# Grid values turned on TensorE instead of by DMA, with the last half chunk of the down projection stacked

## The chip, the cores and the metric

The kernel runs on one core of a Trainium2 chip, in one launch. The metric is device time in microseconds; before, the median of three runs is 670.58 us (665.73 to 671.05). The engines are TensorE (PE; PEld is its weight load), VectorE (DVE), ScalarE (ACT), GpSimd (POOL) and SyncE (SP), which only issues DMAs here. Each takes its own instructions in program order; semaphores tie them together.

## The reference

All tokens (4 batches of 2048, width 256) are normalised; then one branch is a linear attention and the other a gated feed-forward net whose inputs and weights are rounded to FP4 in blocks of 16.

```python
def fp4_quant_dequant(x):
    xb = x.reshape(shape[:-1] + (shape[-1] // BLOCK, BLOCK))
    scale = jnp.maximum(jnp.max(jnp.abs(xb), axis=-1, keepdims=True) / 6.0, 1e-12)
    xn = xb / scale
    idx = jnp.searchsorted(_MID, jnp.abs(xn))
    return (_GRID[idx] * jnp.sign(xn) * scale).reshape(shape)

xn = _layernorm(x)
# attention on xn
Q, K, V = xn @ Wq.T + bq, xn @ Wk.T + bk, xn @ Wv.T + bv
Q, K = Q / norm(Q over tokens), K / norm(K over tokens)
tailor = 1 / (L + Q . (sum(K) + EPS))
s = xn + gamma * (sum(V) + Q (K V)) * tailor
# feed-forward: fp4_linear rounds both operands with fp4_quant_dequant
h = silu(fp4_linear(xn, w_gate)) * fp4_linear(xn, w_up)      # 256 -> 704
g = silu(fp4_linear(h, w_down))                              # 704 -> 256
out = x + s * g
```

## The kernel before

The 8192 tokens are 32 groups of 256 (T = 2 halves of 128 tokens; 8 groups make a batch). The order of the work is written out by hand: the program order is each engine's queue. After a start that also rounds and turns the weights, a loop `for s in range(3, N - 1)` (line 1042) makes 28 passes, each of which works on several groups at once:

- group s+3: gram matrix (`gram_step`), maxima and rounding of its normalised tokens (in `scale_h(s - 1, s + 3)`, together with group s-1), turning of the tokens for the attention (`turn_xn`)
- group s+2: its rounded tokens are scaled back (`rescale_x`, line 488) and split into three parts of a reduced format (`part_a` on ScalarE, `part_b` and `part_m` on VectorE, lines 497 to 511)
- group s+1: gate and up projection in six chunks, each a `gu_begin` (first matmuls, then a scaling copy in PSUM on ScalarE, line 540) and a `gu_end` (last matmuls, Silu, product with up: h). Chunks 0 to 3 have the product on VectorE (`times_up`), 4 and 5 on GpSimd (line 567). The chunks rotate through three PSUM banks
- group s-1: `scale_h` (maxima, reciprocal, product y, lines 163 to 186), `short_part` (three ScalarE copies to 16 bits, line 221), `on_grid` (rounding by a huge addition, line 231)
- group s-2: `rescale_h` (line 513), grid values times scales, in the layout that the down projection needs
- group s-3: `down`, the down projection (line 578), and its Silu `gate_of`
- group s-7: attention output (`preset`, `attend`), one pass later `close` (product with the gate, sum with x) and `store`.

Grid values are made with tokens on partitions, and the next matmul needs them turned. The values and their scales go separate ways. The values: `turn_q` (line 481) has SP issue a DMA transpose of the 16-bit tile into `qt`. The scales: `turn_scales` (line 457) turns them on TensorE, evicts them (`sct`), stores them to DRAM (`there`), and `spread_scales` (line 468) reads them back with each row repeated 16 times, into `se` (128 x 1920, f32, 960 KB, one buffer). `rescale_h` and `rescale_x` multiply `qt` by `se`, on VectorE and on GpSimd. The scales of group s-1 are spread after `rescale_h(s - 2)` has read the old ones.

A group has 1408 h values per token pair (11 chunks of 128; 5.5 per half of the tokens). `down` runs 6 chunks for each half, with the middle chunk in both and half of its weight rows set to zero: 12 matmuls of 128x256 in f32, each of which the profile shows as two instructions.

PSUM tile tag `tp` has two banks for everything that is turned. In every second pass `deviation_steps` yields 13 small VectorE operations (Newton's square root for two groups' deviations, ending in `shiftp`), which `little()` hands out one by one between other work; `normalize(s + 4)` on ScalarE needs them. The attention matrices of a batch are made by a generator, `attention(b)` (line 661), of which `turn()` takes a step at five places of a pass.

Of the kernel before, what the change touches and what calls it, by code (L numbers as in the profile page):

```python
# [9 lines left out]
F32 = mybir.dt.float32  # L10
BF16 = mybir.dt.bfloat16
# [9 lines left out]
BLK = 16  # L21
# [8 lines left out]
def kernel(  # L30
# [31 lines left out]
    P = 128  # L62
# [78 lines left out]
    load_x(4)  # L141
    wd_n = tok.tile([P, NS * P], F32, tag="se", name="wd_n", bufs=1)[:, 0:HF]
    nc.sync.dma_start(
# [6 lines left out]
    ident = const.tile([P, P], F32, tag="ident", name="ident")  # L150
    make_identity(nc, ident)
    nc.gpsimd.memset(wv_sb[:, :, L + 1 : L + 2], 1.0)

# [62 lines left out]
    def grid_tile(y: bass.AP, nm: str):  # L216
        return tok.tile([P, NS * P], F16, tag="t", name=f"t_{nm}", bufs=2)[:, 0 : y.shape[1]]

# [215 lines left out]


    scales, there_sc, spread_sc, turned = {}, {}, {}, {}

# [30 lines left out]
    def spread_scales(key, tag: str = "se"):  # L468
        there, n = there_sc.pop(key)
        most = NS * P if tag == "se" else HF  # L470
        se = tok.tile([P, most], F32, tag=tag, name=f"se_{key}", bufs=1 if tag == "se" else 3)[:, 0 : n * BLK]
        nc.sync.dma_start(
            se,
            there[0:n, :]
            .rearrange("(b g) t -> b (g t)", b=CB)
            .unsqueeze(1)
            .to_broadcast([CB, BLK, n * BLK]),
        )
        spread_sc[key] = se

    def turn_q(n: int, q: bass.AP, tag: str = "qt"):
        F = q.shape[1]
        most = NS if tag == "qt" else NIC
        qt = tok.tile([P, most, P], F16, tag=tag, name=f"qt_{n}", bufs=2 if tag == "qt" else 3)
        nc.sync.dma_start_transpose(qt[:, 0 : F // P, :], q)
        turned[n] = qt.rearrange("p g t -> p (g t)")

    def rescale_x(n: int, key: int):

        f = tok.tile([P, T * L], F32, tag="f", name=f"f_{n}", bufs=2)  # L490
        nc.gpsimd.tensor_tensor(f, turned[key][:, HF:], spread_sc[key][:, HF:], ALU.mult)  # L491
        return f
# [19 lines left out]

    def rescale_h(n: int, lo: int = 0, hi: int = HF, tag: str = "hqt"):
        if lo == 0:
            ht = tok.tile([P, HF], F32, tag=tag, name=f"hqt_{n}", bufs=1 if tag == "hqt" else 3)
            hqt[n] = ht.rearrange("p (g t) -> p g t", t=P)
        ht = hqt[n].rearrange("p g t -> p (g t)")
        nc.vector.tensor_tensor(ht[:, lo:hi], turned[n][:, lo:hi], spread_sc[n][:, lo:hi], ALU.mult)  # L518
        if hi == HF:
            turned.pop(n), spread_sc.pop(n)  # L520

# [54 lines left out]
    hqt, ods = {}, {}  # L576

    def down(n: int, part: int, parts: int = 2, banks=None):

        half = NIC // T  # L580
        t, i = divmod(part, parts)
        if n not in ods:
            ods[n] = ps_od.tile([P, T, L], F32, tag="od", name=f"dn_{n}")
        size = (half + 1) // parts
        for i in range(i * size, (i + 1) * size):
            nc.tensor.matmul(  # L586
                ods[n][:, t, :],
                hqt[n][:, t * half + i, :],
                wdt[:, t * (half + 1) + i, :],
                start=(i == 0),  # L590
                stop=(i == half),
            )

    def gate_of(n: int):
# [66 lines left out]
    def attention(b: int):  # L661
# [7 lines left out]
        nc.tensor.transpose(ps[:, 0:P], S[:, 0, P:L], ident)  # L669
        evict(S[:, 1, 0:P], ps[:, 0:P])  # L670
        u_b = alg.tile([P, L], F32, tag="row", name=f"ub_{b}", bufs=2)
        spread_rows(u_b, S[:, :, L], f"u{b}")
        yield


# [5 lines left out]
        for i, (pool, tag) in enumerate(  # L681
            ((ps_tp, "tp"), (ps_tp, "tp"), (ps_gu, "gu"), (ps_od, "od"))
        ):
# [38 lines left out]
        yield  # L722
        yield


        for t in range(KC):
            nc.vector.tensor_scalar(Q[:, t, :], Q[:, t, :], inv[:, t : t + 1], None, ALU.mult)
        yield
        ps = ps_tp.tile([P, KC, L], F32, tag="tp", name=f"pq_{b}")
# [6 lines left out]
        evict(R, ps)  # L736
        yield
        yield
# [46 lines left out]
        for t, ps in enumerate(pts):  # L785
# [5 lines left out]
            nc.vector.tensor_scalar(MT[:, t, rest], ps[:, rest], tg[:, t : t + 1], None, ALU.mult)  # L791
        yield

        ps = ps_tp.tile([P, KC, L], F32, tag="tp", name=f"pM_{b}")
# [49 lines left out]

    wdt = const.tile([P, NIC + 1, L], F32, tag="wdt", name="wdt")

    def turn_d(wdz):
        half = NIC // T
        H = P // 2
        ends = small.tile([P, KC, P], F32, tag="ends", name="ends", bufs=1)  # L850
        w3 = wdz.rearrange("p (t f) -> p t f", t=KC)
        nc.scalar.copy(ends[:, :, 0:H], w3[:, :, FF - H : FF])
        nc.scalar.copy(ends[:, :, H:P], w3[:, :, 0:H])
        nc.gpsimd.memset(wdt[H:P, half, :], 0.0)
        nc.gpsimd.memset(wdt[0:H, half + 1, :], 0.0)
        for i in range(0, NIC - 1, 2):
            tp = ps_tp.tile([P, 512], F32, tag="tp", name=f"tp_d{i}")
            at = [i + k if i + k < half else i + k + 2 for k in range(2)]
            for k in range(2):
                f0 = at[k] * P if at[k] < half else (at[k] - half - 2) * P + H  # L860
                for t in range(KC):
                    nc.tensor.transpose(
                        tp[:, k * L + t * P : k * L + (t + 1) * P], w3[:, t, f0 : f0 + P], ident
                    )
            if at[1] == at[0] + 1:
                evict_over_one(wdt[:, at[0] : at[0] + 2, :].rearrange("p i n -> p (i n)"), tp)
            else:
                for k in range(2):
                    evict_over_one(wdt[:, at[k], :], tp[:, k * L : (k + 1) * L])
            yield  # L870
        tp = ps_tp.tile([P, 512], F32, tag="tp", name="tp_d")
        for t in range(KC):
            nc.tensor.transpose(tp[:, t * P : (t + 1) * P], ends[:, t, :], ident)
        evict_over_one(wdt[0:H, half, :], tp[0:H, 0:L])
        evict_over_one(wdt[H:P, half + 1, :], tp[H:P, 0:L])
        yield
# [116 lines left out]
    turn_xq(4, rounded(s_x, tx))  # L993
    turn_q(0, on_grid(th, "h0"))
    next(parts)
# [11 lines left out]
    turn_scales(1)  # L1007
    rescale_h(0)
    spread_scales(1)
    turn_q(1, on_grid(th, "h1"))  # L1010

# [10 lines left out]
    def close(f: int):  # L1022
        gated(f, ready.pop(f))
        finish(f, nc.vector)

# [16 lines left out]
    for s in range(3, N - 1):  # L1042
# [11 lines left out]
        turn()  # L1054
        u0 = gu_begin(*pairs[0])
        if s % 2 and s > 3 and s + 4 < N:
            small_ones = deviation_steps()
        sums = sums_of(s + 6)
        for h in late:
            times_up(h)  # L1060
        if parts_x:
            xs = rescale_x(s + 2, s - 2)
        y_h = scale_h(s - 1, s + 3)
        little()
        th = grid_tile(y_h, f"h{s - 1}")
# [24 lines left out]
        if s > 3:  # L1090
            turn_scales(s - 1)
        u2 = gu_begin(*pairs[2])
        if s == 3:
            h1 = gu_end(u1)
            shorts()
        little()
        little()
        if s > 3:
            h1 = gu_end(u1, 1 in DIRECT)
        times_up(h1)  # L1100
        little()
        turn()
        down(s - 3, 0 if s == 3 else 2)
        down(s - 3, 1 if s == 3 else 3)
        q = on_grid(th, f"h{s - 1}")
        little()
        turn_q(s - 1, q)
        if f >= 0:
            preset(f)
        u3 = gu_begin(*pairs[3])  # L1110
        if s == 3:
            down(0, 2)
            down(0, 3)
            turn_scales(2)
        gate_of(s - 3)
        h2 = gu_end(u2, s > 3 and 2 in DIRECT)
        times_up(h2)
        little()
        u4 = gu_begin(*pairs[4])
        h3 = gu_end(u3, s > 3 and 3 in DIRECT)  # L1120
        if parts_x:
            part_a(s + 2, xs)
        times_up(h3)
        little()
        rescale_h(s - 2)
        little()
        spread_scales(s - 1)
        if parts_x:
            part_b(s + 2, xs)
            part_m(s + 2, xs)  # L1130
        little(20)
        if f >= 0:
# [30 lines left out]
    for i in range(f + 3, N):  # L1163
        x_last[i] = x_sb[i]
    y_h = scale_h(n - 1)
    for i in range(5):
# [4 lines left out]
    attends(f)  # L1171
    rescale_h(n - 2, tag="h")
    spread_scales(n - 1)
    turn_q(n - 1, on_grid(th, f"h{n - 1}"))
    downs(n - 2)
# [6 lines left out]
    spread_scales(n, "h")  # L1182
    turn_q(n, on_grid(th, f"h{n}"))
    attends(f + 3, f + 4)
    preset(f + 5, *banks[0])
    rescale_h(n - 1)
    close(f + 1)
    close(f + 2)
# [8 lines left out]
    attends(f + 6, f + 7)  # L1197
    rescale_h(n, 0, (NIC // T + 1) * P, tag="h")
    rescale_h(n, (NIC // T + 1) * P)
    close(f + 5)  # L1200
# [50 lines left out]
```

## Time and profile before

| | us |
|---|---|
| median of three runs | 670.58 |
| the profiled execution, run | 673.65 |
| its span | 671.9 |
| TensorE busy, matmul / weight load | 610.2 / 494.4 |
| VectorE / ScalarE / GpSimd busy | 478.2 / 397.0 / 146.9 |
| granted TensorE clock, mean | 0.979 |

The page shows one profiled execution. "Busy" is the time in which an engine executes; a matmul's end is modelled. A group of instructions is written as line, engine, operation, result <- sources, shapes, count, then busy time, mean ns of one, and idle time before it with what ended it. Four groups that the change touches:

```profile
L586 PE MATMUL dn<-wdt,hqt 128*128 128x256 f32 x768 | 180.4, 379 | 0.5 <-ACT gate L1207 0.5
...
L491 POOL TENSOR_TENSOR f<-qt,se 128x512 f32<-128x512 f16 x27 | 35.4, 1312 | 199.0 <-DMA se<-there 114.0
...
L518 DVE TENSOR_TENSOR hqt<-qt,se 128x1408 f32<-128x1408 f16 (+2 forms) x33 | 53.0, 1607 | 15.1 <-DMA qt<-t_h 15.1
```

Matmuls overlap, so the 379 ns of a `dn` instruction are longer than the distance of two starts.

### The profile page before, as it was taken

To read this page: it belongs to the slowest core of one execution; us is meant where nothing else is said; L and a number is where in the kernel's file an instruction comes from. 1 tells how busy PE (TensorE), PEld (TensorE's weight loads), DVE (VectorE), ACT (ScalarE), POOL (GpSimd) and SP (SyncE) were. 2 spreads that over 40 slices of the span, in tenths; PEclk is the share of its full clock that TensorE was granted. 3 is DMA by queue.
4 is the path that set the end of the run, shared out by engine and by line. 5 is a ranking of instruction groups with operands and counts; after the bars stand their busy time and mean duration, and the time that the engine had idled before them with its cause. 6 is when DMAs were issued, how large, how long until landed. Compare 5 with 4: busy or idle time off the path is not lost.

```text
span 671.9 us, 8659 instructions
## 1 busy us (share of the span) xinstructions
PE 610.2 (91%) x2805; PEld 494.4 (74%) x2807; DVE 478.2 (71%) x915; ACT 397.0 (59%) x1033; POOL 146.9 (22%) x224
## 2 busy tenths in 40 slices
PE   4899996898899999998899999998899999999997
PEld 2445564677778787777778787877778888787785
DVE  6667667584867777687867777687767777687763
ACT  2467847555567676745567685745658575644520
POOL 5467638211011111101012111110111111110000
PEclk9799997897999999999999999999999999999999
DMA  9210475423545756436545656547535545534585
GB/s 211 75 33 16 53 103 128 88 53 77 106 99 123 143 132 142 115 87 136 111 108 124 144 127 141 114 109 131 106 98 128 128 106 125 120 95 96 144 125 135
DMA packets 85513, 74.47 MB, mean 111 GB/s; under 512 B 63228, under 2 KB 69596, under 8 KB 85468
## 3 DMA queue, kind: packets, MB, share of 16 engines
q1 hardware_dynamic: 85196, 73.66, 51.3%
q8 instruction: 22, 0.36, 0.3%
q10 hardware_dynamic: 272, 0.26, 0.1%
q14 instruction: 23, 0.19, 0.1%
HBM read 48.57 MB, written 10.27 MB: 88 GB/s over the span
## 4 chain that ended last, share of the span: by engine, by line
PE 64%; DVE 17%; ACT 10%; DMA 4%; issue 4%; POOL 2%; SPq 0%; ACTq 0%; DVEq 0%; POOLq 0%
PE dn L586 22%; PE gu L536 19%; PE gu L550 6%; PE at L624 5%; PE gram L392 5%; DVE hqt L518 3%; DMA qt<-t_h 3%; PE px L686 2%; DVE xq L510 2%; ACT si L560 2%; ACT gu L540 2%; ACT xn L367 2%; DVE y_h L186 2%; DVE xq L504 2%; DVE scs L163 1%
## 5 line engine op out<-in xcount | busy, mean ns | idle before, releaser
L536 PE MATMUL gu<-wgu,xq 128*128 128x512 f32 (+1 forms) x640 | 185.5, 412 | 7.0 <-ACT xq L499 5.2
L586 PE MATMUL dn<-wdt,hqt 128*128 128x256 f32 x768 | 180.4, 379 | 0.5 <-ACT gate L1207 0.5
L540 ACT ACTIVATE gu<-gu 128x512 f32<-128x512 f32 (+1 forms) x160 | 89.2, 557 | 139.6 <-PE gu L536 139.0
L586 PEld LDWEIGHTS dn<-wdt,hqt 128*128 128x128 f32 x768 | 143.8, 190 | 22.6 <-issue 1.4
L536 PEld LDWEIGHTS gu<-wgu,xq 128*128 128x128 f32 x640 | 116.3, 191 | 29.7 <-ACT xq L499 5.4
L571 DVE TENSOR_TENSOR h<-si,gu 128x256 f32<-128x256 f32 x108 | 45.4, 420 | 119.8 <-ACT si L560 119.6
L567 POOL TENSOR_TENSOR h<-si,up 128x192 f32<-128x192 f32 (+1 forms) x84 | 64.5, 773 | 258.6 <-ACT up L566 241.3
L550 PE MATMUL gu<-wgu,xq 128*128 128x512 f32 (+1 forms) x320 | 99.6, 392 | 0.4 <-ACT gu L540 0.4
L560 ACT ACTIVATE si<-gu 128x256 f32<-128x256 f32 (+1 forms) x192 | 70.0, 364 | 28.2 <-PE gu L536 19.2
L491 POOL TENSOR_TENSOR f<-qt,se 128x512 f32<-128x512 f16 x27 | 35.4, 1312 | 199.0 <-DMA se<-there 114.0
L392 PE MATMUL gram<-xn 128*128 128x257 f32 (+1 forms) x256 | 52.3, 350 | 18.9 <-ACT xn L367 18.9
L392 PEld LDWEIGHTS gram<-xn 128*128 128x128 f32 x256 | 45.6, 203 | 31.4 <-ACT xn L367 23.5
L221 ACT ACTIVATE t_h<-y_h 128x704 f16<-128x704 bf16 (+2 forms) x86 | 60.8, 769 | 10.2 <-DVE y_h L186 9.6
L550 PEld LDWEIGHTS gu<-wgu,xq 128*128 128x128 f32 x320 | 59.5, 189 | 9.6 <-ACT gu L540 1.1
L518 DVE TENSOR_TENSOR hqt<-qt,se 128x1408 f32<-128x1408 f16 (+2 forms) x33 | 53.0, 1607 | 15.1 <-DMA qt<-t_h 15.1
L624 PE MATMUL at<-M,xnt 128*128 128x256 f32 x256 | 63.6, 378 | 0.0
L536 PE MATMUL gu<-wp,xqt 128*128 128x512 f32 (+1 forms) x120 | 52.9, 588 | 2.8 <-ACT xqt L379 2.2
L186 DVE SCALAR_TENSOR_TENSOR y_h<-h,inv_h 128x1408 f32<-128x1408 f32 x32 | 52.9, 1652 | 1.1
L624 PEld LDWEIGHTS at<-M,xnt 128*128 128x128 f32 x256 | 47.9, 189 | 6.2
L163 DVE TENSOR_REDUCE scs<-h 128x88 f32<-128x1408 f32 x32 | 51.6, 1612 | 0.0
L367 ACT ACTIVATE xn<-x,shiftp,rstdp 128x256 f32<-128x256 f32 x46 | 25.4, 604 | 31.5 <-DVE shiftp L343 31.5
L536 PEld LDWEIGHTS gu<-wp,xqt 128*128 128x128 f32 x120 | 22.9, 199 | 24.7 <-issue 16.5
(166 smaller groups left out, 742.1 us busy)
## 6 DMA issues: line engine op xcount, KB each, us to landing
se<-there SPq DMA_DIRECT2D x27, 960.0 KB
x<-in_L_attn_x_dram SPq DMA_DIRECT2D x32, 256.0 KB
out_dram<-gate SPq DMA_DIRECT2D x31, 256.0 KB
xl<-in_L_attn_x_dram SPq DMA_DIRECT2D x27, 256.0 KB
se<-there SPq DMA_DIRECT2D x5, 704.0 KB
there<-sct SPq DMA_DIRECT2D x27, 60.0 KB
wd_n<-in_L_ffn_w_down_dram SPq DMA_DIRECT2D x1, 704.0 KB
wgu_n<-in_L_ffn_w_up_dram SPq DMA_DIRECT2D x2, 256.0 KB
```

What stands on the lines that cost most here:

```text
L163: nc.vector.tensor_reduce(sc, src.rearrange("p a (n k) -> p a n k", k=BLK), AX.X, ALU.max, apply_absolute_value=True)
L186: nc.vector.scalar_tensor_tensor(y.rearrange("p (a n k) -> p a n k", a=a, k=BLK), src.rearrange("p a (n k) -> p a n k", k=BLK), DOWN, inv. ...
L221: nc.scalar.activation(t[:, lo:hi], upper[:, lo:hi], AF.Copy, scale=ONE * (1.0 + 2.0**-8))
L392: nc.tensor.matmul(grams[b][:, o : o + L + 1 - c * P], xn[:, t, c * P : (c + 1) * P], xn[:, t, c * P : L + 1], start=(g == 0 and t == 0 an ...
L518: nc.vector.tensor_tensor(ht[:, lo:hi], turned[n][:, lo:hi], spread_sc[n][:, lo:hi], ALU.mult)
L536: nc.tensor.matmul(gu[:, : nb * P], x_k, w_k, start=(k == 0), stop=(k == len(pairs) - 1), skip_group_check=True)
L540: nc.scalar.activation(gu[:, : nb * P], gu[:, : nb * P], AF.Copy, scale=1.0 + 1.0 / STEP)
L550: nc.tensor.matmul(gu[:, : nb * P], xqt[n][2][:, t, c, :], wgu[2][:, c, cols], start=False, stop=(c == KC - 1), skip_group_check=True,)
L560: nc.scalar.activation(si[:, :nb, :], pair[:, :, 0, :], AF.Silu)
L567: nc.gpsimd.tensor_tensor(h, si[:, :nb, :], up[:, :nb, :], ALU.mult)
L586: nc.tensor.matmul(ods[n][:, t, :], hqt[n][:, t * half + i, :], wdt[:, t * (half + 1) + i, :], start=(i == 0), stop=(i == half),)
L624: nc.tensor.matmul(ready[n][:, t, :], xnt[n][:, c, t * P : (t + 1) * P], M[:, c, :], start=False, stop=(c == KC - 1), skip_group_check=True,)
```

## The change

DMA transposes are gone. `turn_chunks` turns up to eight 128x128 chunks of the 16-bit grid values on TensorE into a `tp` bank, and `rescale_x` and `rescale_h` read them from PSUM; `rescale_x` thereby moves from GpSimd to VectorE. `turned[n]` now holds the untransposed tile.

```diff
-    def turn_q(n: int, q: bass.AP, tag: str = "qt"):
...
-        nc.sync.dma_start_transpose(qt[:, 0 : F // P, :], q)
-        turned[n] = qt.rearrange("p g t -> p (g t)")
+    def turn_chunks(q: bass.AP, g0: int, g1: int, nm: str) -> bass.AP:
+        tp = ps_tp.tile([P, 1024], BF16, tag="tp", name=f"tp_q{nm}_{g0}")
+        for g in range(g0, g1):
+            o = (g - g0) * P
+            nc.tensor.transpose(tp[:, o : o + P], q[:, g * P : (g + 1) * P].bitcast(BF16), ident16)
+        return tp[:, 0 : (g1 - g0) * P].bitcast(F16)
...
-        nc.gpsimd.tensor_tensor(f, turned[key][:, HF:], spread_sc[key][:, HF:], ALU.mult)
+        nc.vector.tensor_tensor(f, turn_chunks(turned[key], NIC, NS, f"x{n}"), spread_sc[key][:, HF:], ALU.mult)
...
+    def rescale_h(n: int, tag: str = "hqt"):
...
+        for g0, g1 in ((0, 8), (8, NIC)):
+            cols = slice(g0 * P, g1 * P)
+            nc.vector.tensor_tensor(
+                ht[:, cols], turn_chunks(q, g0, g1, f"h{n}"), spread_sc[n][:, cols], ALU.mult
+            )
```

`se` has two buffers. `down` runs five whole f32 chunks for each half of the tokens; the middle chunk's two halves are split by `part_middle` into a short part and its rest, stacked over each other (`both`), and multiplied by two 128x256 weight tiles `wde` of the reduced format: 10 f32 matmuls and 4 of the reduced format in place of 12.

```diff
+    def part_middle(n: int, engine):
...
+        for t in range(T):
+            nc.scalar.activation(both[sides[t], t, :], middle[sides[t], :], AF.Copy, scale=SHORT)
+        for t in range(T):
+            engine.tensor_tensor(
+                both[sides[1 - t], t, :],
+                middle[sides[t], :],
+                both[sides[t], t, :].bitcast(F32),
+                ALU.subtract,
+            )
+        over_lower[n] = both
...
+        if i == half - 1:
+            for k in range(2):
+                nc.tensor.matmul(
+                    ods[n][:, t, :],
+                    over_lower[n][:, t, :],
+                    wde[:, k, t, :],
...
-        finish(f, nc.vector)
+        finish(f, nc.gpsimd)
```

In the loop, the scales are spread right after they were turned; `rescale_x` stands before `scale_h`, as before, but now on VectorE; the parts and the Newton steps come earlier. Pass 3 keeps the later places for the parts.

```diff
         u0 = gu_begin(*pairs[0])
+        if s > 3:
+            part_middle(s - 3, nc.gpsimd)
...
-        if parts_x:
+        if parts_x and s > 3:
             xs = rescale_x(s + 2, s - 2)
         y_h = scale_h(s - 1, s + 3)
-        little()
+        little(3)
...
         if s > 3:
             turn_scales(s - 1)
+            spread_scales(s - 1)
         u2 = gu_begin(*pairs[2])
...
-        little()
-        little()
+        little(3)
         if s > 3:
             h1 = gu_end(u1, 1 in DIRECT)
+        if parts_x and s > 3:
+            part_a(s + 2, xs)
         times_up(h1)
-        little()
+        little(2)
         turn()
...
         q = on_grid(th, f"h{s - 1}")
-        little()
-        turn_q(s - 1, q)
+        little(20)
+        turned[s - 1] = q
...
         times_up(h2)
-        little()
+        if parts_x and s > 3:
+            part_b(s + 2, xs)
+            part_m(s + 2, xs)
         u4 = gu_begin(*pairs[4])
         h3 = gu_end(u3, s > 3 and 3 in DIRECT)
-        if parts_x:
+        if parts_x and s == 3:
+            xs = rescale_x(s + 2, s - 2)
             part_a(s + 2, xs)
         times_up(h3)
-        little()
         rescale_h(s - 2)
-        little()
-        spread_scales(s - 1)
-        if parts_x:
+        if parts_x and s == 3:
             part_b(s + 2, xs)
             part_m(s + 2, xs)
-        little(20)
```

In `attention`, the spreading of u moves one step later, the pauses around Q, R and M are placed anew, and the four tiles of px take od, gu, tp, tp in place of tp, tp, gu, od. After the loop `rescale_h` of the last group is one call, and `part_middle` runs on VectorE after each `rescale_h`. `turn_d` builds `wde` from the two half chunks of the weights instead of zero-padded rows.

## The prediction

> **What bounds the kernel now.** I read the page's busy shares first, then the waits, then the chain of waits and the timeline of two middle passes of the loop (503 to 538 us), then the DMA rate by stretches.
>
> ```profile
> PE 610.2 (91%) x2805; PEld 494.4 (74%) x2807; DVE 478.2 (71%) x915; ACT 397.0 (59%) x1033; POOL 146.9 (22%) x224
> ```
>
> ```profile
> POOL f L491 <- DMA se<-there: 114.0, 16, 9.4
> ...
> PE gram L392 <- ACT xn L367: 18.9, 11, 6.9
> ```
>
> TensorE is the wall: 91% busy, and in the chain of waits its pieces lie end to end. The gram of one pass starts at 520.29 and the next at 538.05, 17.76 us, of which 1.29 us is idle before the second; so a pass without a gap is 16.47 us of TensorE. That gap comes in every second pass (nine of 1.23 to 1.31 us, 11.6 us in sum), behind the Newton steps, which VectorE ends after rescale_h and the parts. The first line of the waits (who waited for what: us in all, times, longest) is the one that I build on: GpSimd waits 114 us in all for the spread scales `se`, and it costs nothing, because GpSimd is 22% busy and the parts of x are wanted only at the end of the pass.
>
> ```profile
> 518.36 0.62 SPq L472 DMA_DIRECT2D se<-there  x1
> 519.04 0.45 SPq L649 DMA_DIRECT2D out_dram<-gate  x1
> 519.54 0.42 SPq L108 DMA_DIRECT2D xl<-in_L_attn_x_dram  x1
> 527.61 0.34 SPq L465 DMA_DIRECT2D there<-sct  x1
> ```
>
> ```profile
> 512.23 1.16 POOL L491 TENSOR_TENSOR f<-qt,se 128x512 f32<-128x512 f16 x1 [5.92 <-DMA se<-there]
> ```
>
> The scales of this pass left for DRAM at 527.61; `se` is issued only after the old one has been read. GpSimd's f at 512.23 was released by the `se` issued at 500.42: 11.8 us. The same difference over the sixteen waits runs from 11.40 us (issue 126.17, start 137.57) to 12.30 us (399.88, 412.18).
>
> ```profile
> 525.00:529.00 4.00, 4.00 (x20) 3.39 (x19) 3.02 (x10) 3.86 (x10) 0.00 (x0) 1.00 0.54 122
> 93.00:98.00 5.00, 5.00 (x20) 3.48 (x19) 3.45 (x5) 2.12 (x5) 0.00 (x0) 1.00 0.53 120
> ```
>
> The last two figures are DMA share and GB/s. With little else in flight `se` moves at 120 to 122 GB/s; at that rate its 960 KB (983 kB) take 8 us, whatever else is quiet.
>
> **TensorE's own sum.** *Down projection*: 24 instructions a group become 20, and 4 single-pass ones of 256 columns are added. The old ones take 0.216 us each (six in 1.29 to 1.30 in the chain): minus 0.86. The gate/up matmuls in the same format take 0.93 for four of 512 columns and 0.70 for four of 384, so 0.116 for 256: plus 0.47; at worst the weight load's 0.19 each: plus 0.76. I take minus 0.40. *Turning the grid values*: 15 transposes a pass. Nearest row: tp_xn, four 4-byte 128x128 transposes in 0.44 us, 0.11 each, taken as the upper end; half of it, 0.055, if two bytes halve the passes. I take 0.07: 1.05 us (0.83 to 1.65). Pass: 16.47 - 0.40 + 1.05 = 17.1 us (16.9 to 18.0).
>
> The Trainium skill ("TensorE: Matmul & The Clock Gate", Part 4: PE-mode transpose) gives about 275 ns for a 16-bit 128x128 transpose inside a kernel, and speaks against this change: by it the 15 would be an estimated 4.1 us and the pass 20.2. The rows here say 0.11 for a wider type, and I go by the rows.
>
> **The other moves.** Newton steps: the eight that stood before rescale_h or later now end after on_grid, so shiftp is there before normalize; the gaps of 11.6 us go. Attention gaps (eleven waits on Q, MT and xnt from 129 to 630 us) are 19 us in sum; between none and all goes, I take 12. close's second add (0.69 us on VectorE) goes to GpSimd, at 1.2 to 2 us by its own 128x512 rows; what is behind it there is the next h product, which came 9 us after the gate's product (525.79, 534.86), so it costs nothing; without that gap it would delay h by its own length. rescale_x goes to VectorE: GpSimd's row is 1.18, VectorE's product with one PSUM operand of 128x512 is 0.68, of 128x256 is 0.42; I take 0.7. rescale_h in two pieces costs one more start, by the rows of 512 and 1408 columns (0.69, 1.62) 0.16 us. part_middle: two ScalarE copies of 64x128, below the 0.27 of the 120x128 row, and two small GpSimd products; about 0.5 us of ScalarE, which has 4 us free in a pass. part_a/b/m are the same instructions earlier. VectorE thus stays at about 14 of 17 us in busy time; the trouble is order, not load.
>
> **The new wait.** rescale_x stands at the head of VectorE's pass, before scale_h, and VectorE takes its queue in order. It needs the `se` that was issued in the pass before, and that issue needs: scale_h of that pass (VectorE, behind its own rescale_x), the three short copies (ScalarE), the scales' eviction (behind them on ScalarE), the trip to DRAM, and `se`. Every pass therefore contains one whole round:
> - rescale_x: 0.7
> - scale_h, from the reduction's start (519.81) to the end of y_h's first part (523.25 + 1.62): 5.06
> - ScalarE from the first short copy (525.43) to the end of sct (527.31 + 0.27): 2.15
> - `there` to the next issue on SP: 1.55 at 637.67 to 639.22, 2.00 at 102.35 to 104.35; I take 1.6
> - `se` from issue to use: 11.4 to 12.3. In the new order of SP, store, x and xl follow it at once, as at 518.36, so the rows apply. I take 11.4, the lowest of the sixteen, since no transposes share the engines any more. Alone: the 704 KB one issued at 639.22 was through by about 646.5 (1.8 us to start, then about 130 GB/s); 983 kB at that rate give 9.4, the lower end
> - hand-overs: 0.2
>
> Sum: 21.1 us a pass (19.1 with `se` alone, 22.0 at 12.3), against TensorE's 17.1. Queued behind the waiting rescale_x are scale_h, h0, gated and every later VectorE step; behind y_h on ScalarE stand the scaling copy and si of the next chunks, so TensorE stops at tp_sc and at the second end of a chunk. TensorE's 4 us of slack then hides transposes, attention and gaps: gain and loss on TensorE no longer count. The second buffer of `se` lets the issue go some 6 us earlier, but the use moves up by more: f started at 530.09 in a pass whose u0 began at 519.36, 10.7 us in; it now stands about 1.2 us in.
>
> The Trainium skill ("DMA: Bandwidth & Descriptors", Rules for kernel authors) says to issue a DMA early and wait for it late. The rows agree in kind: a late wait on an idle engine cost nothing here for 114 us.
>
> **Sum against the profiled execution** (span 671.9, run 673.65, which is 0.5% above the median 670.58). Start: with the DMA transposes gone SP is free (their issues took 6.75 and 2.85 us), the scales of group 2 can leave at 97.4 instead of 102.35, `se` lands near 109.5, and tp_sc of pass 4 comes 3.2 us later (0.7 + 2.46 from reduction to scaled maxima): 112.7, before 115.3. From there 25 passes to tp_sc of pass 29 took 597.13 - 115.3 = 481.8 (19.3 each, attention included); at 21.1 they take 527.5. So 45.7 - 2.6 = 43.1 more. Tail: for the last three groups the transposes stand on TensorE right where hqt was ready before: 3 x 0.77; twice the rescaling (1.8) has no cover (n-2 before its down, n before its down); less 4 x 0.4 saved: plus 4.3. 671.9 + 47.4 = 719.3 span, 721.1 run, **718** on the scale of the median.
>
> **Rivals.**
> 1. *`se` lands uncontended* (9.4): round 19.1. tp_sc 29 at 590.2; the attention passes, 22.1 us before with 5.8 us of gaps in three, stay TensorE-bound near 20.7 and add about 16. Time 606.2 - 597.1 + 4.3 more, **684** by the median. For it: share 0.54 leaves room beside `se`. Against: all sixteen rows, with the same neighbours.
> 2. *The round does not bind; the change is faster.* It decides where `se` lands within 7.4 us of its issue (17.1 less the 9.7 of the other steps). Then 671.9 - 11.6 (Newton) - 12 (attention) - 5 (the 5.17 us gap at 106, behind a DMA transpose) + 28 x 0.43 (transposes at 0.055) + 4.3 = 660, **659** by the median; 667 with transposes at 0.07 and half of the attention gaps left. For it: 704 KB took 7.3 us in the tail, and the removed transposes were most of the small packets. Against: 122 GB/s in stretches without transposes.
> 3. *TensorE's transposes are dear* (0.11 or above): pass 18.0; hidden under 21.1, and in rival 2's case 28 x 1.25 in place of 28 x 0.43 makes 681.
>
> **Chances.** Round binds, contended 0.55 (718; 700 to 742); uncontended 0.20 (684); round does not bind 0.20 (659, of which a third ends within 1%); dearer than 742 0.05. Faster by over 1% 0.15, within 1% (about what a measurement can tell) 0.07, slower 0.78. The range reaches into rival 2 at 660 and up to 742.
>
> **What would show it.** Right: VectorE's f waits on DMA se<-there in nearly every pass, 3 to 5 us each; gram to gram 19 to 22 us in plain passes; TensorE below 87% with idle before tp_sc; the gram<-xn gaps gone. Wrong: f released by the transposes on TensorE, `se` landing under 8 us, passes of 17 us. A 0.25 us spacing of the new transposes would show the third rival.

## The result, and the profile after

After takes 733.59 us (median of 4 runs, 732.69 to 736.31) against 670.65 us before: the ratio is 1.0964, with a 95% interval of 1.0905 to 1.1022. The profiled execution took 733.18 us, its span is 731.3 us, the mean granted clock 0.972.

The page of after: first the busy line, then the shares of the chain that ended last by engine and by line, then three groups (line, engine, operation, result <- sources, shapes, count, then busy us, mean ns of one, and idle time ahead with its releaser).

```profile
PE 639.2 (87%) x3267; PEld 512.4 (70%) x3269; DVE 472.5 (65%) x950; ACT 419.0 (57%) x1100; POOL 167.6 (23%) x283
...
DMA 36%; PE 28%; DVE 26%; ACT 7%; issue 3%; POOL 1%; DVEq 0%; SPq 0%; ACTq 0%; POOLq 0%
...
L498 DVE TENSOR_TENSOR f<-tp_qx,se 128x512 f32<-128x512 f16 x27 | 18.7, 692 | 130.6 <-DMA se<-there 120.5
...
L526 DVE TENSOR_TENSOR hqt<-tp_qh,se 128x1024 f32<-128x1024 f16 x64 | 53.9, 883 | 21.3 <-PE tp_qh L492 21.3
...
L616 PE MATMUL dn<-wdt,hqt 128*128 128x256 f32 x640 | 159.9, 392 | 2.7 <-DVE hqt L526 2.2
```

TensorE is busy 29 us more than before, but the span is 59 us longer: its share falls from 91% to 87%. Little of the 29 us is added work: x_columns_first (below) has the same matmuls and is busy 614.2 us, at a mean granted clock of 0.999. The chain of before, over its whole span, was TensorE for 64%:

```profile
PE 64%; DVE 17%; ACT 10%; DMA 4%; issue 4%; POOL 2%; SPq 0%; ACTq 0%; DVEq 0%; POOLq 0%
```

Now it is TensorE for 28%, and 36% go to DMA and 26% to VectorE. VectorE has no more to do than before (472.5 against 478.2 us); it stands still for 130.6 us ahead of one instruction a pass, `f`.

The waits of after (who waited for what: us in all, times, longest):

```profile
DVE f L498 <- DMA se<-there: 120.5, 22, 7.2
ACT t_h L227 <- DVE y_h L188: 93.9, 25, 6.6
...
PEld tp_sc L468 <- issue: 49.0, 16, 4.8
PE tp_sc L468 <- DVE scs L174: 46.3, 16, 4.7
```

The first line is the wait that GpSimd had before, for nearly the same sum (114.0 us), now on VectorE. The others are those who wait for VectorE: ScalarE for `y_h`, TensorE for the scaled maxima. These sums overlap and are not added.

The chain of after from 394.76 to 415.96 us (start, us, what; pieces of one engine left out):

```profile
382.83 11.83 DMA se<-there
...
394.76 0.69 DVE f L498
395.45 2.13 DVE scs L165 x2
...
397.86 0.92 DVE inv_h L178
...
398.80 2.23 DVE y_h L188 x2
...
404.28 11.59 DMA se<-there
...
415.96 0.69 DVE f L498
```

This is one whole round: `f` to `f` in 21.20 us, and over half of it is one transfer. What SP does between, from its timeline (start, us, operation):

```profile
402.64 0.34 SPq L472 DMA_DIRECT2D there<-sct  x1
404.28 0.60 SPq L479 DMA_DIRECT2D se<-there  x1
404.98 0.42 SPq L690 DMA_DIRECT2D out_dram<-gate  x1
405.45 0.41 SPq L100 DMA_DIRECT2D x<-in_L_attn_x_dram  x1
405.91 0.45 SPq L108 DMA_DIRECT2D xl<-in_L_attn_x_dram  x1
```

Between `y_h` and the store lie ScalarE's short copies and the eviction (400.46 to 402.62); the trip to DRAM takes 1.64 us. From the `f` of pass 4 (112.65) to that of pass 29 (651.59) 25 rounds take 538.94 us, 21.56 each.

### The profile page after: what moved, and what is told of

The parts are those of the page before. It is cut to its first block, busy times and chain, and to the rows that moved or that the text cites. A ratio compares the mean times of both kernels' runs of the same rounds, so it can differ in the third digit from the quotient of the medians.

```text
span 731.3 us, 9674 instructions
## 1 busy us (share of the span) xinstructions
PE 639.2 (87%) x3267; PEld 512.4 (70%) x3269; DVE 472.5 (65%) x950; ACT 419.0 (57%) x1100; POOL 167.6 (23%) x283
## 4 chain that ended last, share of the span: by engine, by line
DMA 36%; PE 28%; DVE 26%; ACT 7%; issue 3%; POOL 1%; DVEq 0%; SPq 0%; ACTq 0%; POOLq 0%
DMA se<-there 35%; PE gu L545 10%; DVE scs L165 6%; PE dn L616 6%; DVE y_h L188 5%; PE at L665 3%; DVE inv_h L178 3%; DVE f L498 2%; PE gu L559 2%; ACT t_h L227 2%; DVE h L580 1%; DVE isq_yp L347 1%; PE pa L788 1%; ACT si L569 1%; PE tp_qh L492 1%
## 5 line engine op out<-in xcount | busy, mean ns | idle before, releaser
L545 PE MATMUL gu<-wgu,xq 128*128 128x512 f32 (+1 forms) x640 | 183.9, 410 | 6.6 <-DVE h L580 5.9
L616 PE MATMUL dn<-wdt,hqt 128*128 128x256 f32 x640 | 159.9, 392 | 2.7 <-DVE hqt L526 2.2
L616 PEld LDWEIGHTS dn<-wdt,hqt 128*128 128x128 f32 x640 | 124.8, 199 | 24.1 <-issue 2.9
L576 POOL TENSOR_TENSOR h<-si,up 128x192 f32<-128x192 f32 (+1 forms) x84 | 56.9, 681 | 247.6 <-ACT up L575 247.5
L559 PE MATMUL gu<-wgu,xq 128*128 128x512 f32 (+1 forms) x320 | 104.4, 408 | 1.6 <-ACT gu L549 1.1
L498 DVE TENSOR_TENSOR f<-tp_qx,se 128x512 f32<-128x512 f16 x27 | 18.7, 692 | 130.6 <-DMA se<-there 120.5
L682 POOL TENSOR_TENSOR gate<-gate,xl 128x512 f32<-128x512 f32 x27 | 34.5, 1280 | 224.6 <-issue 199.1
L526 DVE TENSOR_TENSOR hqt<-tp_qh,se 128x1024 f32<-128x1024 f16 x64 | 53.9, 883 | 21.3 <-PE tp_qh L492 21.3
L398 PE MATMUL gram<-xn 128*128 128x257 f32 (+1 forms) x256 | 50.2, 340 | 8.3 <-ACT xn L373 8.3
L398 PEld LDWEIGHTS gram<-xn 128*128 128x128 f32 x256 | 42.3, 195 | 14.5 <-ACT xn L373 9.0
L468 PE MATMUL tp_sc<-ident,scs 128*120 128x128 f32 (+1 forms) x32 | 9.7, 304 | 46.3 <-DVE scs L174 46.3
```

Source lines behind the costliest of these rows:

```text
L398: nc.tensor.matmul(grams[b][:, o : o + L + 1 - c * P], xn[:, t, c * P : (c + 1) * P], xn[:, t, c * P : L + 1], start=(g == 0 and t == 0 an ...
L526: nc.vector.tensor_tensor(ht[:, cols], turn_chunks(q, g0, g1, f"h{n}"), spread_sc[n][:, cols], ALU.mult)
L545: nc.tensor.matmul(gu[:, : nb * P], x_k, w_k, start=(k == 0), stop=(k == len(pairs) - 1), skip_group_check=True)
L559: nc.tensor.matmul(gu[:, : nb * P], xqt[n][2][:, t, c, :], wgu[2][:, c, cols], start=False, stop=(c == KC - 1), skip_group_check=True,)
L576: nc.gpsimd.tensor_tensor(h, si[:, :nb, :], up[:, :nb, :], ALU.mult)
L616: nc.tensor.matmul(ods[n][:, t, :], hqt[n][:, t * (half + 1) + i, :], wdt[:, t * half + i, :], start=(i == 0), stop=False, skip_group_chec ...
```

## The experiments

| kernel | us, median | ratio to before, 95% interval |
|---|---|---|
| after | 733.6 | 1.0964 (1.0905 to 1.1022) |
| before_x_on_vector | 871.5 | 1.3016 (1.2971 to 1.3060) |
| x_after_scale | 662.1 | 0.9890 (0.9848 to 0.9933) |
| x_columns_first | 654.6 | 0.9776 (0.9747 to 0.9806) |
| neighbours_early | 717.9 | 1.0722 (1.0690 to 1.0753) |
| sixteen_rows | 667.4 | 0.9965 (0.9934 to 0.9996) |
| x_first_turned_twice | 680.5 | 1.0175 (1.0139 to 1.0210) |
| x_first_old_down | 663.1 | 0.9917 (0.9888 to 0.9945) |
| x_first_newton_old | 669.2 | 0.9984 (0.9957 to 1.0011) |
| x_first_and_after | 659.5 | 0.9847 (0.9822 to 0.9872) |
| before_newton_early | 649.7 | 0.9694 (0.9677 to 0.9711) |
| dma_turned_old_down | 642.2 | 0.9587 (0.9555 to 0.9620) |
| dma_turned_stacked | 637.8 | 0.9524 (0.9498 to 0.9550) |

The theory: `rescale_x` at the head of VectorE's pass makes a round through `se`, and this alone makes after slower than before. The rivals: the transposes on TensorE, the stacking or the moved steps.

### Is it the place of rescale_x?

**before_x_on_vector** changes one word of before: `rescale_x` runs on VectorE. No transposes, no stacking, one buffer for `se`.

```diff
-        nc.gpsimd.tensor_tensor(f, turned[key][:, HF:], spread_sc[key][:, HF:], ALU.mult)
+        nc.vector.tensor_tensor(f, turned[key][:, HF:], spread_sc[key][:, HF:], ALU.mult)
```

> The kernel before with one word changed: rescale_x on VectorE in place of GpSimd, everything else as it was, DMA transposes included. Theory: here se is issued only after rescale_h, so the round is longer than in the changed kernel: rescale_x 0.7, from scale_h's start to rescale_h's end 11.2 (its VectorE work) to 15.5 us (502.79 to 518.29 in the trace before), se 11.8: 24 to 28 us a pass against 19.3, and 790 to 900 us. If the wait for se costs nothing because later work hides it (rival), the kernel loses at most VectorE's 0.7 us a pass, 27 x 0.7 = 19: 670 to 690 us.

871.5 us. Its waits:

```profile
ACT t_h L221 <- DVE y_h L186: 225.4, 28, 17.2
DVE f L491 <- DMA se<-there: 223.2, 26, 12.0
```

The wait that was free on GpSimd costs 202 us on VectorE. It is more than in after because, with one buffer, the next `se` is issued only behind `rescale_h`: in the middle of the trace `hqt` starts at 510.71, the issue is at 512.36, `f` at 524.32. A round takes 26.84 us on average here (`f` at 121.89 to `f` at 792.91) and 21.56 in after: the change's second buffer and its early spreading win back a good part of what its own move costs. The granted clock is also lower, 0.894 and 0.902 in the two runs for 0.984 to 0.989 in before's beside them; how much of the 202 us is TensorE at that clock is not shown.

**x_after_scale** is after, with two lines exchanged.

```diff
+        y_h = scale_h(s - 1, s + 3)
         if parts_x and s > 3:
             xs = rescale_x(s + 2, s - 2)
-        y_h = scale_h(s - 1, s + 3)
```

> The changed kernel with two lines exchanged: rescale_x stands behind scale_h in VectorE's queue. If the round over the spread scales sets the pass (theory), it is cut: scale_h, the short copies and the issue of se no longer wait for the se before. TensorE then sets a plain pass: 16.47 - 0.39 + 15 x 0.057 = 16.9 us, and with the attention's extra work 18.2 to 18.6 on average, so the time falls by 25 x 3 to 25 x 3.4, to 648 to 660 us. If TensorE's added transposes, or the clock it loses in its gaps, make the change slow (rival), the exchange moves nothing there: 715 to 735 us.

662.1 us, just above what was expected, 71 us below after. From its waits, and two neighbouring grams of TensorE's timeline:

```profile
DVE f L498 <- DMA se<-there: 2.3, 4, 1.0
```

```profile
356.21 1.53 PE L398 MATMUL gram<-xn 128*128 128x257 f32 x8
...
373.25 1.53 PE L398 MATMUL gram<-xn 128*128 128x257 f32 x8
```

`f` hardly waits for `se`; TensorE is 94% busy, and its plain passes (gram to gram) take 17.05 us. scale_h no longer stands behind the wait of its own pass, only behind that of the pass before. So a round through `se` has two passes to run in, and no longer sets their length. The order of the two lines is worth more than the whole loss of 63 us.

**x_columns_first** leaves the order and makes the transfer short: the 512 columns that `f` needs are read first, by a DMA and into a tile of their own.

```diff
+        if n * BLK > HF:
+            sx = tok.tile([P, T * L], F32, tag="sx", name=f"sx_{key}", bufs=2)
+            nc.sync.dma_start(sx, rows[:, HF:].unsqueeze(1).to_broadcast([CB, BLK, T * L]))
+            spread_x[key] = sx
...
+        nc.sync.dma_start(se, rows[:, 0:HF].unsqueeze(1).to_broadcast([CB, BLK, HF]))
```

> The changed kernel with se read in two DMAs: the 512 columns for x first, into a tile of their own, then the 1408 for h. rescale_x keeps its place ahead of scale_h. Theory: only the landing in the round gets shorter: 256 KB at 122 GB/s, 2.1 us, and some 2 to 3 to start and end, so 4 to 5 in place of 11.7; the round is 9.5 + 4 to 5 = 13.5 to 14.5 us, below TensorE's 16.9, and the time is that of the exchanged order, 648 to 662 us. If the order of VectorE itself were at fault and not the landing (rival), it stays above 710 us.

654.6 us. The timeline of VectorE in a plain pass, and the wait for `f` in the list:

```profile
350.67 0.69 DVE L496 TENSOR_TENSOR f<-tp_qx,sx 128x512 f32<-128x512 f16 x1 [1.91 <-PE tp_qx L490]
```

```profile
DVE f L496 <- PE tp_qx L490: 46.4, 22, 2.8
```

`f` is released by TensorE's transposes now, in step with a pass of 17.05 us. The issue of `sx` was at 343.13, so the scales were there within 7.5 us; whether in the 4 to 5 us expected can't be seen from a wait that TensorE ended. TensorE is the wall again, and the kernel is 2.2% faster than before.

### Why does the read take 11.7 us?

**neighbours_early** issues the store and the loads of x and xl from ScalarE's queue, ahead of its short copies, so that they don't follow `se`.

```diff
-        load_x(s + 7)
-        reload_x(s - 7)
...
+            load_x(s + 7, nc.scalar)
+            reload_x(s - 7, queue=nc.scalar)
+            store(nc.scalar)
...
-        store()
```

> The changed kernel with the loads of x and xl and the store issued from ScalarE's queue just ahead of the short copies, when se has landed and the next one is not yet issued; the round itself is untouched. If the three neighbours stretch se's landing (part of the theory), it falls from 11.7 to 9.4 to 9.9 us, the pass from 21.6 to 19.3 to 19.8, and the time by 25 x 1.8 to 25 x 2.3, to 676 to 690 us (three more issues stand on ScalarE, outside the round or with 1.5 us inside it: then up to 715). If se is slow by its own shape alone (rival), the landing stays above 11 us and the time within 10 us of 733.

717.9 us, between theory and rival: a miss for both. `se`, issued at 417.71, is used at 428.42: 10.7 us, 1 us less than with neighbours. The stretches of that transfer (window, then busy us of PE, PEld, DVE, ACT and POOL with counts, granted clock, DMA share, GB/s):

```profile
420.00:425.00 5.00, 5.00 (x31) 4.38 (x30) 2.73 (x5) 3.63 (x13) 0.65 (x2) 1.00 0.51 114
425.00:427.00 2.00, 2.00 (x13) 1.79 (x12) 0.00 (x0) 1.36 (x4) 1.27 (x3) 1.00 0.56 123
427.00:428.40 1.40, 1.40 (x8) 1.13 (x7) 0.00 (x0) 0.30 (x1) 0.17 (x1) 1.00 0.01 0
```

Two things stand here. The windows count a packet (one piece of a transfer) where it starts; by the trace's packets the last of `se` ends at 427.37, and another 1.05 us pass before `f` starts. And a lone `se` keeps the sixteen DMA engines only half busy, 0.51 to 0.56.

**sixteen_rows** follows the second. The read repeats 8 rows of DRAM 16 times; here the scales are stored twice, and 16 rows are repeated 8 times. The same bytes land in the same tile.

```diff
-        there = dram.tile([NS * CB, P], F32, tag="there", name=f"there_{key}")
-        nc.sync.dma_start(there[0:n, :], st[0:n, :])
+        there = dram.tile([2 * CB, NS, P], F32, tag="there", name=f"there_{key}")
+        copies = there.rearrange("(b c) g t -> c b g t", c=2)
+        for c in range(2):
+            nc.sync.dma_start(copies[c][:, 0 : n // CB, :], st[0:n, :])
...
-            .to_broadcast([CB, BLK, n * BLK]),
+            .to_broadcast([2 * CB, BLK // 2, n * BLK]),
```

> After, with the turned scales stored twice, so that the read of se is 16 outer rows repeated 8 times in place of 8 rows repeated 16 times: the same bytes into the same tile. In stretches with se alone the DMA engines are busy 0.51 to 0.55 of sixteen at 114 to 123 GB/s, as if eight of them carried it. Theory: they do (the Trainium skill, DMA: Bandwidth & Descriptors, Rules for kernel authors, says that an outermost dimension below 16 confines a DMA to so many engines), so the read moves at up to twice the rate. 983 kB then take some 4 us of moving for 8, se is there 7.7 to 9 us after its issue for 11.7, the second store adds 0.4, the round is 17.4 to 19 and the time 640 to 680 us. Rival: the rate is that of the one source row or of the queue, the share means something else: se still 11 us or more, 725 to 745 us.

667.4 us: 66 us off after, with rescale_x where the change put it and the whole `se` in one read. SP, and the stretches of the read, of this kernel:

```profile
384.65 1.34 SPq L474 DMA_DIRECT2D there<-sct  x2
387.63 0.56 SPq L481 DMA_DIRECT2D se<-there  x1
```

```profile
387.60:389.40 1.80, 1.80 (x18) 1.70 (x18) 1.64 (x4) 0.78 (x3) 0.00 (x0) 1.00 0.32 102
389.40:391.00 1.60, 1.60 (x11) 1.50 (x10) 1.60 (x4) 1.03 (x4) 0.03 (x1) 1.00 1.04 254
391.00:392.00 1.00, 1.00 (x8) 0.93 (x7) 0.41 (x1) 0.97 (x4) 0.57 (x1) 1.00 1.02 230
```

`f` starts at 394.19: 6.6 us after the issue, where after needs 11.7, and all the engines are busy. In the trace a packet of `se` takes about as long in both kernels, 0.58 us (neighbours_early) and 0.52 us at the median; but some 8 are under way at a time there and some 16 here, and the whole read moves in 4.4 us for 8.3. So the read ran on eight of the sixteen because its outermost dimension was 8. The Trainium skill ("DMA: Bandwidth & Descriptors", Rules for kernel authors) states it: an outermost dimension below 16 confines a DMA to at most that many engines. The runs agree: 0.51 and 114 GB/s with 8 rows, 1.04 and 254 with 16. The second store is dearer than expected: from the first store to the issue of `se` it is 2.98 us against 1.64. The round is then 17.4 us (394.19 to 411.62), still 0.4 above TensorE's pass of 17.05, and `f` still waits:

```profile
DVE f L500 <- DMA se<-there: 47.1, 16, 4.1
```

### What do the other parts cost?

Next to x_columns_first, where TensorE is the wall, parts of the change can be priced.

**x_first_turned_twice** does each transpose of grid values twice, into the same place.

```diff
-        for g in range(g0, g1):
+        for g in list(range(g0, g1)) * 2:
```

> The version with the x columns of the scales read first (654.6 us), with every transpose of the grid values done twice into the same place. Theory: TensorE is the wall there and a transpose costs what the chain shows, 0.057 us, so 15 more a pass are 0.86 us and 28 passes with the tail about 26 us: 674 to 686, plain passes of 17.9 us. Rival (transposes are dearer than their spacing shows, 0.11 or more each): 700 or above, passes of 18.7 us or more.

680.5 us, 25.9 more, with plain passes of 17.89 us. A line of TensorE's timeline in after and one in this kernel (11 transposes and 22):

```profile
405.54 0.79 PE L492 MATMUL tp_qh<-ident,t_h 128*128 128x128 bf16 x11
406.17 1.08 PE L665 MATMUL at<-M,xnt 128*128 128x256 f32 x4
```

```profile
555.03 1.40 PE L490 MATMUL tp_qh<-ident,t_h 128*128 128x128 bf16 x22
556.27 1.08 PE L663 MATMUL at<-M,xnt 128*128 128x256 f32 x4
```

Start to start: 0.63 us for 11 and 1.24 for 22, 0.057 and 0.056 each; the pass says (17.89 - 17.05) / 15 = 0.056.

**x_first_old_down** undoes the stacking.

```diff
-        for i in range(i * size, min((i + 1) * size, half)):
+        for i in range(i * size, (i + 1) * size):
...
-        if i == half - 1:
-            for k in range(2):
...
-    wde = const.tile([P, 2, T, L], F32R, tag="wde", name="wde")
```

> The version with the x columns of the scales read first (654.6 us), but with the down projection as before: 12 f32 matmuls of 256 columns a group, no part_middle, the zero-padded weight rows. Theory: TensorE is the wall again in this version, so the stacking is worth its matmuls, 24 x 0.216 - (20 x 0.216 + 4 x 0.117) = 0.39 us a group, 32 groups 12.5 us: 664 to 670 us. Rival: the stacking is hidden or eaten by the parts it adds, 652 to 658.

663.1 us, 8.5 more and just under the range; the plain pass is 17.43 us, 0.38 more. The pass agrees with 0.39; the medians are 4 us short of 12.5. The start is one part of this: the split weight tiles add gaps of 1.07, 0.64 and 0.58 us on TensorE, which this kernel hasn't but for one of 0.49, and a gram that starts at 124.22 in x_columns_first starts at 122.71 here. Where the rest goes is not shown: the two traced executions lie 12.5 us apart (spans 652.4 and 664.9), but the one of this kernel was the slowest of its four, 666.7 us for 663.0 to 663.1.

**x_first_newton_old** puts the Newton steps back.

```diff
-        little(3)
+        little()
...
-        little(20)
+        little()
```

> The version with the x columns of the scales read first (654.6 us), with the Newton steps handed out in the old places of the loop. Theory: the gaps before gram come back in the passes that end with them, seven to nine of about 1.3 us: 661 to 668 us, and gram<-xn waits of 8 us or more in the list. Rival: VectorE's order is so different that they end in time anyway, 653 to 657.

669.2 us, 14.6 more and above the range (its ten runs spread from 664.2 to 671.9). The way was not the expected one: gram hardly waits in plain passes (17.10 and 17.38 us for 17.05); the longest new gaps, 2.7 us, stand ahead of the transposes of three attention passes, behind ScalarE's `xnt`, and ScalarE itself waits:

```profile
ACT xn L373 <- DVE shiftp L349: 21.7, 12, 2.4
```

The granted clock is a part of it. Its record has 0.5 for 3.4 us in four places of this loop (from 147.06, 300.66, 324.55 and 478.15) and nowhere in that of x_columns_first, and over the ten runs the time goes with the mean clock, from 664.2 us at 0.994 to 671.9 us at 0.983.

**x_first_and_after** applies both cures.

```diff
+        y_h = scale_h(s - 1, s + 3)
...
-        y_h = scale_h(s - 1, s + 3)
```

> The x columns of the scales are read first, and rescale_x stands after scale_h. Both cures at once: the round has 4.3 us for it from the order and some 4 us from the smaller read. Theory: either alone already takes the round below TensorE's pass of 17.05, so the second adds nothing but VectorE's order: 648 to 657 us. Rival: the read still binds somewhere and the two add up: below 645.

659.5 us, above both expectations: 4.9 us worse than x_columns_first (3.2 by the spans of the traced executions, both at a mean clock of 0.999). Plain passes stay at 17.05; passes with attention steps grow (24.52 us for 23.79, twice). Once the scales are early, `f` at the head of the pass is the better place; why is not shown.

### What is the change worth without its turning?

**before_newton_early** is before with the Newton steps in the new places.

```diff
-        little()
+        little(3)
...
-        little()
+        little(20)
```

> Before, with only the Newton steps handed out early, as after has them. Theory: the nine gaps before gram, 11.6 us in sum, go and nothing else moves: 657 to 663 us, every plain pass 16.5 us. Rival: the steps delay h, on_grid and so the DMA transposes, and the gaps come back in another place: 666 to 675.

649.7 us, below the expected range: 20 us better where the gaps were 11.6 us. Plain passes go from 17.91 and 16.57 in turn to 16.46, but passes with attention gain as well, the first three 5.9 us in the traces (71.0 to 65.1). Those go with the granted clock, the column after POOL's busy time. Two stretches of before, and of this kernel at about the same work:

```profile
128.40:135.20 6.80, 6.16 (x14) 4.87 (x15) 3.37 (x16) 1.43 (x4) 1.50 (x2) 0.50 0.62 133
152.30:159.10 6.80, 5.80 (x19) 4.97 (x20) 6.57 (x12) 4.16 (x12) 0.59 (x1) 0.50 0.59 128
```

```profile
126.80:133.60 6.80, 6.30 (x31) 5.53 (x32) 5.68 (x21) 1.86 (x4) 1.36 (x2) 1.00 0.59 128
147.80:154.60 6.80, 6.08 (x33) 5.34 (x33) 6.41 (x9) 3.10 (x10) 0.60 (x1) 1.00 0.60 137
```

13.6 us at half the clock cost an estimated 6.8 us at most. In both kernels TensorE stops 2.8 us at the first of these stretches (until 129.04 and 127.30), so the length of that stop does not decide. The mean clock is 0.992 to 0.996 in this kernel's runs and 0.984 to 0.987 in before's beside them; why the earlier steps raise it is not shown.

**dma_turned_old_down** adds to this the attention's new places.

```diff
-            ((ps_tp, "tp"), (ps_tp, "tp"), (ps_gu, "gu"), (ps_od, "od"))
+            ((ps_od, "od"), (ps_gu, "gu"), (ps_tp, "tp"), (ps_tp, "tp"))
```

> The version with DMA transposes and all the rest of the change (637.8 us), with the down projection as before. Theory: TensorE's matmuls count fully here, so the stacking is worth 32 x 0.39 = 12.5 us less what part_middle exposes in the tail and at the start (1.8 us): 647 to 651 us, plain passes 16.5 us. Rival: the stacking gives nothing (637 to 640), and the gain is all Newton and attention.

642.2 us, below the 647 expected: on top of the early Newton steps the attention's places are worth 7.5 us, and the stacking less than its matmuls, as the next kernel shows.

**dma_turned_stacked** adds the stacked down projection: the whole change, except that the values are turned by DMA, GpSimd rescales x, close's second add is on VectorE, and the parts of x and the spreading of the scales (one buffer) stand in their places of before. Against x_columns_first:

```diff
-        nc.vector.tensor_tensor(f, turn_chunks(turned[key], NIC, NS, f"x{n}"), spread_x.pop(key), ALU.mult)
+        nc.gpsimd.tensor_tensor(f, turned[key][:, HF:], spread_sc[key][:, HF:], ALU.mult)
```

> Before's way of turning (DMA transposes into qt, GpSimd multiplies the x columns, the scales spread after rescale_h into one buffer), with all the rest of the change: stacked down projection, early Newton steps, the attention's new places. Theory: without the round and without transposes on TensorE the pass is 16.47 - 0.39 = 16.1 us; 670.6 less 12.5 (stacking), less 8 to 11 (Newton) and up to 8 (attention) gives 638 to 650 us, faster than every version that turns on TensorE. Rival: the DMA transposes hold SP and the queues, and the moved steps make hqt late: 655 to 668.

637.8 us, just under the range, 4.8% faster than before and the best of all. GpSimd and SP in a plain pass of it, from the two timelines:

```profile
483.97 1.17 POOL L491 TENSOR_TENSOR f<-qt,se 128x512 f32<-128x512 f16 x1 [6.89 <-DMA se<-there]
```

```profile
483.38 2.57 SPq L485 DMA_TRANSPOSE qt<-t_h  x1
488.28 0.62 SPq L472 DMA_DIRECT2D se<-there  x1
```

The same wait of seven microseconds for the same scales is back, and is free. Plain passes are 16.07 us, 0.39 less than with the old down projection; of 12.5 us only 4.3 arrive in the medians. In the traces the start takes 1.7 us more, and the first attention pass 25.14 us for 21.81: there TensorE stops 1.85 us for `both`, which GpSimd makes, and right behind it the granted clock is 0.5 for 3.4 us (from 115.04), as it is not with the old down projection. In the next pass TensorE stops 2.81 us for an h (2.07 with the old down projection).

Against x_columns_first, where TensorE turns the values without a round, this kernel is 16.8 us faster, and its plain pass is 0.98 us shorter; 15 transposes of 0.057 are 0.86 of that. So turning on TensorE costs time here even when nothing waits for the scales, though the two kernels also differ in the places of the parts and of close's second add.

## Why the prediction was right, point by point

**The new wait.** Right, in mechanism and place, shown from both sides: the move alone on before costs 202 us, and taking `scale_h` out from behind it wins back 71. Its signs came in kind, two of them not in size: `f` waits for `se` in 22 passes, but 5.5 us on average and not 3 to 5; TensorE is at 87.4%, where less than 87% was forecast, with most of its idle time in the loop ahead of `tp_sc`. Plain passes take mostly 20.5 to 22.4 us, and there are no gram gaps after the start.

**The round.** 21.1 us predicted, 21.20 in the round shown. Its terms: scale_h 5.06 as predicted, ScalarE 2.16 for 2.15, the trip 1.64 for 1.6. The term that was mis-sized is `se` from issue to use: the prediction took 11.4, the lowest of its rows, "since no transposes share the engines any more"; it is 11.7 in the round shown and 11.8 on average of the 22 waits, which makes 10 us in 25 rounds. That the shown round meets the sum so closely is partly luck: its hand-overs take almost nothing, where the sum had 0.2. The transposes' sharing was not what made the transfer long; eight engines were. The mean of 25 rounds is 21.56, as three of them, with attention steps, took 22.80, 23.26 and 23.27: these give 6.0 us, the other 22, at 21.35, 5.4 us, 11.4 in all above 25 x 21.1.

**The sum.** Span 719.3 predicted, 731.3 measured. The loop missed by 11.4. At the start `f` of pass 4 was expected near 109.5 and came at 112.65: the scales of group 2 left at 99.41, not 97.4, and trip and `se` took 13.2 us. From the last `f` to the end it is 79.7 us, 2.6 less than the sum had. 11.4 + 3.1 - 2.6 makes the 12 us.

**TensorE's own sum.** Down 0.40 less a pass: 0.38 and 0.39 measured. Transposes 0.07 each: 0.057, near the lower end. The pass without a round: 17.1 predicted, 17.05 measured. The 16.47 that it starts from took one gram where the chain's piece begins (520.29) and not where it starts (520.13); start to start, before's passes without a gap take 16.57, and only before_newton_early's take 16.46. Each transpose stays 0.216 to 0.231 us in the records of x_columns_first, but they overlap, and a row of them costs 0.057 apiece. The figure of the Trainium skill ("TensorE: Matmul & The Clock Gate", Part 4: PE-mode transpose), some 275 ns, fits the stay of one better than its price in a row; by it the doubling would have cost an estimated 4.1 us a pass, and it cost 0.84.

**Rival 1** (`se` uncontended in 9.4 us, time 684) was mis-sized: without neighbours it is 10.7, and the time 717.9. Its 9.4 ended with the last bytes and left out the 1.05 us from there to the use, and it had 130 GB/s, where 119 moved (983 kB in 8.3 us). Nor was its row alone: a DMA transpose was issued 0.66 us behind that `se`.

**Rival 2** (the round does not bind, 659, or 667 with less of the gains) is what x_columns_first and x_after_scale show, 654.6 and 662.1. Its point of decision was `se` within 7.4 us of its issue: with 6.6 in sixteen_rows the round still takes 17.4, since the second store adds 1.3 us to it, and so it still decides plain passes, by 0.4 us.

**Rival 3** (transposes dear) falls with the doubling.

**Newton and attention gains** were put at 11.6 and 12. On before they are 20.2 and 7.5; the sum, 27.7 for 23.6, came out nearly right by luck: the split was not, and a part of the 20.2 is the granted clock, which the prediction did not reckon with. That TensorE's slack in a round hides gain and loss alike in after, as predicted, is argued: no run takes one of these steps out of after.

## What to carry to other kernels

When a step moves to another engine, its waits move with it: a wait that is free at the end of an idle queue becomes the loop's period if it stands at the head of a queue that also feeds the next transfer; add up that round before the engines' busy time. The moved steps and the stacking were worth 32 us by themselves; the round hid this, and with the round gone the transposes on TensorE still took about half of it. Trying the parts alone found a kernel 4.8% faster. And when a transfer is in the round, look at the DMA share beside its rate: half busy engines meant a shape that used half of them.

## What was not expected of the hardware

- A broadcast read with 8 outer rows moves at 114 to 123 GB/s with the DMA share at 0.51 to 0.56; with 16 outer rows the same bytes move at 230 to 254 GB/s with all engines busy.
- From the last packet of `se` to its use about 1 us passes: 1.05 in neighbours_early, 0.96 in after's round, 0.82 in sixteen_rows.
- A stop of two to three microseconds can cost TensorE more than itself, and need not. The stretch of after behind the stop of 3.18 us that ends at 397.97, and four around the stop of 2.90 us that ends at 419.18 (columns as above):

```profile
398.00:401.50 3.50, 3.50 (x18) 3.00 (x18) 3.40 (x7) 1.04 (x2) 0.00 (x0) 1.00 0.00 0
...
416.00:419.00 3.00, 0.28 (x3) 0.08 (x1) 2.96 (x4) 0.54 (x3) 0.00 (x0) 1.00 0.16 62
419.00:422.00 3.00, 2.82 (x9) 2.34 (x10) 2.93 (x4) 0.33 (x1) 0.00 (x0) 0.68 0.00 0
422.00:425.00 3.00, 3.00 (x13) 2.47 (x13) 1.52 (x5) 3.00 (x7) 1.27 (x1) 0.75 0.08 19
425.00:437.00 12.00, 12.00 (x72) 10.34 (x71) 4.28 (x8) 8.14 (x24) 2.09 (x4) 1.00 0.60 129
```

The column after POOL's is the granted clock: 1.00 behind the first stop; 0.68 and 0.75 behind the second, means of stretches in which the clock record has 0.5 from 420.06 to 423.47; then full again. Of the 15 stops of 2.25 to 3.51 us ahead of `tp_sc` between 200 and 640 us, 8 have such a stretch at their end and 7 have none. What decides is not shown. Behind before's 1.30 us gap at 538.05 the clock stayed at 1.00.
